# Turning the token rows of the expert pairs on VectorE and through DRAM instead of on TensorE

## The chip, the core and the metric

The kernel runs on one core of a Trainium2 chip. A core has five engines that run side by side, each with an instruction queue of its own that is worked off in order: TensorE (PE, matmuls; PEld is its loading of the stationary operand), VectorE (DVE), ScalarE (ACT), GpSimd (POOL) and SyncE (SP), which here only issues transfers. Transfers (DMAs) are issued from SP, ACT or POOL, are cut into packets, and are carried by 16 DMA engines that all queues share. A queue's next instruction waits until the semaphores it names have come; so a transfer that waits holds up every transfer issued behind it from the same engine.

The metric is the device time of one launch in microseconds (us), as the median of several runs. All numbers are f32.

## The reference

One block of a gated cross-attention network over 32 sequences of 112 rows (3,584 tokens of width 256):

```python
x = x + tanh(g_xattn) * xattn(ctx_1024, layernorm(x))      # 16 heads of 64, keys: 375 context rows and the 112 own ones
x = x + tanh(g_ffn) * moe(layernorm(x))

def moe(x):                                                # D = 256, F = 1024, E = 8 experts
    s = softmax(x @ gate_w); top2, idx = top_k(s, 2); top2 = top2 / sum(top2)
    h = gelu(einsum('td,edf->etf', x, w1) + b1)
    y = einsum('etf,efd->etd', h, w2) + b2
    return sum over the two chosen experts of top2 * y
```

The kernel does not compute all experts for all tokens: it routes each token to its two experts and computes only these.

## The kernel before, in words

**Attention first.** The first 1,440 us or so are the attention of the 32 sequences, with the gate's scores and the routing of the tokens woven in. Every routed row (a token, once per chosen expert, with its weight and its number behind its 256 values: `C` = 260 columns) is scattered to the DRAM table `xg`, which holds one region per expert. During attention, GpSimd also forms sums and differences of the experts' weights and writes them to DRAM (`ws1`, `ws2`; `piece_in`, `piece_sums`, `piece_out`).

**Then the experts.** The rows of the table are worked off in units. `PAIRS` = 21 units are pairs of 128 rows of one expert (`EARLY` = 13 of them can be located before the last tokens are routed, `LATE` = 8 after), and at least `SURE` = 18 more are single blocks of 128 rows. A pair is two Strassen products: `hidden_pair` (seven products of eight 128x128 matmuls: rows times w1) and `second_pair` (seven such products with w2). Both take half matrices and their sums as operands, so a pair needs the weights `w11`, `s23`, `s1`, `12_22`, `s4` for the first layer and `b11`, `b2x`, `t14`, `t32` for the second, 3.5 MB together. Each has one buffer. A transfer into it is issued from SP (`fetch_first`, `fetch_second`) as soon as the products that read the old weights are done, and it is skipped on the chip when the next pair is of the same expert (the condition `cond`).

**The order is written out by hand.** Each engine's instructions stand in the order in which the Python code calls them. In the loop at lines 1852 to 1875, iteration `t` has, in this order: `hidden_pair(t)`; `fetch_first(t + 1)`; the turning of the next pair's rows, `turn_rows(t + 1)`; `rows_sums(t + 1)` (four differences on GpSimd, tile `xt`); a share of the late routing (`pieces_of`, mostly VectorE); `hidden_sums(t)`; `second_pair(t - 1)` and `out_pair(t - 1)`, whose rows are added to the output by GpSimd's indirect DMAs; `fetch_second(t)`; and `rows_ahead(t)`, which fetches the rows `xs` of pair t + 3 from the table, from SP or (later) from ACT.

**What is turned.** `xs` has a row per partition. As an operand of a product, D must lie on the partitions. `turn_rows` (line 1153) makes `xsT` with four TensorE transposes per pair (two halves of D, two blocks; line 1158) into a PSUM bank, and one copy from there to SBUF, by ScalarE in this loop (line 1162). With this layout, partition p of half k holds column k * 128 + p, and the rows of w1 lie in the same way ("(k p)" in the transfers' patterns).

Attention already has another way to turn rows, for its inputs: `turn_inputs` (32x32 blocks turned by VectorE, line 382), `send_inputs` (to the DRAM tile `turned_in`) and `take_inputs` (back, in runs of 32 values, so that the blocks land turned as a whole; line 397).

The functions that the change touches, and what calls them:

Of the kernel before, what the change touches and what calls it, by code (L numbers as in the profile page):

```python
# [23 lines left out]
def kernel(  # L24
# [20 lines left out]
    nc = tc.nc  # L45
# [79 lines left out]
    turned = [dram.tile([QB, QW, QB, 2 * NCK * 2 * QW], F32, name=f"turned_{n}") for n in range(4)]  # L125
    b1d = dram.tile([E, P, NF], F32, name="b1d")
# [74 lines left out]
    if True:  # L201
# [877 lines left out]
        def half_of_w1(e, k, h):  # L1079
            return w1[bass.ds(e, 1), k * P : (k + 1) * P, h * 512 : (h + 1) * 512].rearrange(  # L1080
                "o p f -> p (o f)"
            )

        def rows_of_w1(e, k):
            return w1[bass.ds(e, 1), k * P : (k + 1) * P].rearrange("o p (h f) -> p (o h) f", h=2)

        def columns_of_w1(e, h):
            return w1[bass.ds(e, 1), :, h * 512 : (h + 1) * 512].rearrange(
                "o (k p) f -> p (o k) f", p=P
            )  # L1090
# [54 lines left out]
        def weights_ahead():  # L1145

            pool = ctx.enter_context(tc.tile_pool(name="wexp", bufs=1, side="right"))
            found["w1"] = pool.tile([P, KD, FF], F32, name="w1_0")
            e, _ = expert_of(0)
            fetch_biases(0, e, pool, 1)  # L1150
            nc.sync.dma_start(found["w1"], w1[bass.ds(e, 1)].rearrange("o (k p) f -> p (o k) f", p=P))

        def turn_rows(t, copy=None):
            n = 2 if t < PAIRS else 1
            ps = psum(KD, n, P)
            for k in range(KD):
                for b in range(n):
                    nc.tensor.transpose(ps[:, k, b, :], xs[t][:, b, k * P : (k + 1) * P], ident)
            xsT[t] = found["tiles" if t > 0 else "early"].tile(
                [P, KD, 2, P], F32, tag="xsT", name=f"xsT_{t}"  # L1160
            )
            (copy or nc.vector.tensor_copy)(xsT[t][:, :, :n, :], ps)

# [248 lines left out]
        def piece_in(n):  # L1412
# [4 lines left out]
            if l == 0:  # L1417

                for h in range(2):
                    lo = h * 512 + c * P  # L1420
                    src = w1[e, :, lo : lo + P].rearrange("(k p) f -> p k f", p=P)
# [430 lines left out]
        for t in range(1, PAIRS):  # L1852
            if t > 1:
# [4 lines left out]
                turn_rows(t + 1, nc.scalar.copy)  # L1858
                if t + 1 < PAIRS:
                    rows_sums(t + 1)  # L1860
            pieces_of(shares.pop(0) if shares else 0)
# [7 lines left out]
            if t + AHEAD == EARLY:  # L1869
                do(outgoing)  # L1870
                del outgoing[:]
            rows_ahead(t)
# [69 lines left out]
```

## Time and profile before

| | |
|---|---|
| median of 3 runs | 1870.04 us (1869.91 to 1871.43) |
| the profiled execution | 1871.91 us, its span 1870.2 us |
| PE busy | 1845.6 us, 99% |
| DVE, ACT, POOL busy | 74%, 60%, 52% |
| DMA | 462.51 MB in 389,747 packets, 247 GB/s on average |
| stage of the pairs | from 1452 us (`hidden_pair(1)`) to 1720 us |
| stage of the single blocks | from 1720 us to the end |

The profile divides the span into 40 slices of 46.8 us; the digit of a slice is a busy share in tenths. DMA's share is the time that packets took, summed over the 16 engines and divided by 16 times the width of the slice; packets of one engine can overlap, so it can be above 1. A timeline line names the start, the duration, the engine, the line of the code, the operation, the tiles (written, then read) and their count, and in square brackets the idle time ahead of it and what ended it. Line numbers are those of the kernel before; behind the change they are a little higher. Iteration t of the pairs' loop is told in the text by the start of `hidden_pair(t)`.

### The profile page before, as it was taken

How to read it: one execution, taken by the hardware profiler on the slowest of the kernel's cores; microseconds unless marked ns; L12 is line 12 of the kernel's file. 1: busy time of each engine (PE TensorE's matmuls, PEld its weight loads, DVE VectorE, ACT ScalarE, POOL GpSimd, SP SyncE). 2: the span in 40 equal slices, each digit the busy share in tenths (PEclk: the TensorE clock that was granted, in tenths of full speed). 3: DMA queues.
4: the chain of work that ended last, by engine and by line, in shares of the span. 5: the costliest groups of instructions: out<-in, count | busy, mean ns of one | idle time of the engine just before them, and what ended most of it. 6: DMA issues, size and time to landing. Idle time of an engine off the chain costs nothing. (4 is left out here: it accounts for less than half of the span.)

```text
span 1870.2 us, 37202 instructions
## 1 busy us (share of the span) xinstructions
PE 1845.6 (99%) x12336; PEld 1410.7 (75%) x12336; DVE 1377.5 (74%) x2898; ACT 1131.2 (60%) x2718; POOL 968.0 (52%) x1359
## 2 busy tenths in 40 slices
PE   8999999999999999999999999999999999999998
PEld 4776777676777677766777777767676999999897
DVE  6888887878887878787878787887776477854111
ACT  4776666756776767666767676666756334344333
POOL 6434342525354846484556655662334588877212
PEclk9999999999999999999999999999999999999999
DMA  6577767666878897989898988887547886897872
GB/s 208 204 244 251 247 215 236 228 211 215 261 263 266 285 288 269 289 280 293 280 282 280 284 279 288 266 300 235 217 171 254 265 242 174 263 349 221 247 201 42
DMA packets 389747, 462.51 MB, mean 247 GB/s; under 512 B 142984, under 2 KB 279472, under 8 KB 373168
## 3 DMA queue, kind: packets, MB, share of 16 engines
q1 hardware_dynamic: 359568, 432.19, 69.6%
q0 software_dynamic: 11328, 15.33, 4.3%
q10 hardware_dynamic: 18656, 12.58, 2.5%
q8 instruction: 99, 1.62, 0.3%
q14 instruction: 96, 0.79, 0.1%
HBM read 316.05 MB, written 186.96 MB: 269 GB/s over the span
## 5 line engine op out<-in xcount | busy, mean ns | idle before, releaser
L592 ACT ACTIVATE ex<-bank,nmx 128x512 f32<-128x512 f32 x512 | 344.0, 698 | 85.0 <-DVE nmx L583 85.0
L606 ACT ACTIVATE ex<-ex,rc 128x512 f32<-128x512 f32 x512 | 345.1, 730 | 59.5 <-DVE rc L603 58.8
L583 DVE TENSOR_REDUCE nmx<-bank 128x1 f32<-128x487 f32 x512 | 298.3, 655 | 73.3 <-PE bank L573 72.8
L611 DVE STREAM_TRANSPOSE ex<-ex 128x1024 f32<-128x1024 f32 x256 | 314.4, 1228 | 20.4 <-ACT ex L606 20.0
L524 POOL TENSOR_TENSOR vv<-tmpv,vv 128x512 f32<-128x512 f32 x64 | 81.9, 1280 | 407.2 <-ACT vv L512 396.4
L573 PE MATMUL bank<-kT,qTs 64*128 64x487 f32 x1024 | 234.4, 584 | 1.2 <-ACT outT L652 0.8
L635 PEld LDWEIGHTS bank<-exT,vv 128*64 128x64 f32 (+1 forms) x4096 | 197.5, 136 | 33.2 <-issue 24.8
L652 ACT COPY outT<-bank 128x256 f32<-128x256 f32 (+3 forms) x160 | 40.0, 314 | 296.0 <-PE bank L635 291.5
L635 PE MATMUL bank<-exT,vv 128*64 128x112 f32 (+1 forms) x4096 | 212.0, 260 | 3.0 <-DMA exT<-turned 3.0
L471 PE MATMUL bank<-tT,wkv_s 128*128 128x487 f32 x378 | 186.5, 576 | 0.5 <-ACT ex L592 0.5
L476 PE MATMUL bank<-wkv_s,tT 128*128 128x256 f32 x768 | 186.5, 379 | 0.0
L476 PEld LDWEIGHTS bank<-wkv_s,tT 128*128 128x128 f32 x768 | 145.8, 190 | 44.0 <-issue 22.1
L1452 POOL TENSOR_TENSOR piece<-piece 128x128 f32<-128x128 f32 x256 | 116.8, 456 | 113.9 <-DMA piece<-in_L_ffn_w_dram 102.7
L573 PEld LDWEIGHTS bank<-kT,qTs 64*128 64x128 f32 x1024 | 98.3, 186 | 96.6 <-issue 70.0
L1207 POOL DMA_INDIRECT out_dram<-y,xs x60 | 93.5, 1558 | 146.2 <-DVE y L1234 63.2
L476 PEld LDWEIGHTS bank<-wkv,kvT 128*128 128x128 f32 x512 | 95.8, 190 | 56.5 <-issue 33.5
L476 PE MATMUL bank<-wkv,kvT 128*128 128x256 f32 x512 | 131.8, 380 | 0.8 <-ACT ex L592 0.6
L471 PE MATMUL bank<-kvT,wkv 128*128 128x487 f32 x252 | 130.1, 598 | 0.0
L521 DVE TENSOR_TENSOR vv<-bank,vv 128x512 f32<-128x512 f32 x192 | 123.6, 669 | 7.7 <-POOL vv L524 7.7
L521 DVE TENSOR_TENSOR kT<-bank,kT 128x487 f32<-128x487 f32 x189 | 116.9, 640 | 15.5 <-PE bank L471 12.7
L1262 ACT ACTIVATE h<-h,b 128x256 f32<-128x256 f32 x160 | 66.0, 495 | 91.4 <-DVE h L1275 64.5
L410 PEld LDWEIGHTS bank<-kvT,wq_sb 128*128 128x128 f32 x512 | 96.8, 190 | 28.1 <-issue 17.0
(299 smaller groups left out, 3654.3 us busy)
## 6 DMA issues: line engine op xcount, KB each, us to landing
turned<-ex SPq DMA_DIRECT2D x128, 1024.0 KB
exT<-turned SPq DMA_DIRECT2D x128, 1024.0 KB
w_t<-ws SPq DMA_DIRECT2D x40, 512.0 KB
w<-in_L_ffn_w_dram SPq DMA_DIRECT2D x38, 512.0 KB
w_b2x<-in_L_ffn_w_dram SPq DMA_DIRECT2D x38, 512.0 KB
ws<-piece SPq DMA_DIRECT2D x64, 256.0 KB
turned_in<-inputs SPq DMA_DIRECT2D x28, 512.0 KB
kvT<-turned_in SPq DMA_DIRECT2D x224, 64.0 KB
```

What stands on the lines that cost most here:

```text
L410: nc.tensor.matmul(ps, lhsT=wq_sb[:, k, i * P : (i + 1) * P], rhs=kvT[g][:, k, :, :S], start=(k == 0), stop=(k == KD - 1),)
L471: nc.tensor.matmul(ps, lhsT=w[:, 0, i * P : (i + 1) * P], rhs=x[:, :NK], start=True, stop=True)
L476: nc.tensor.matmul(ps[:, c, :], lhsT=x[:, (2 * h + c) * P : (2 * h + c + 1) * P], rhs=w[:, 1, i * P : (i + 2) * P], start=True, stop=True,)
L521: nc.vector.tensor_tensor(v[o], ps, v[r], ALU.add)
L573: nc.tensor.matmul(ps[:, :NK], lhsT=qT[b // 2, i][r, b % 2].rearrange("p a i -> p (a i)"), rhs=kT[b, i][r, :], start=True, stop=True,)
L583: nc.vector.tensor_reduce(nmx[b, i][:, j : j + 1], pss[b, i][j][:, :NK], AX.X, ALU.max, negate=True)
L592: nc.scalar.activation(exs[n % EXB][:, :, p, :, j, :], ps[j].rearrange("p (c r k) -> p k c r", c=NCK, r=QW), AF.Exp, bias=nmx[b, i][:, j : ...
L606: nc.scalar.mul(t, t, rc[:, j : j + 1])
L611: nc.vector.transpose(t, t)
L635: nc.tensor.matmul(ps[y * DH : (y + 1) * DH, r, x * S : (x + 1) * S].rearrange("p (a i) -> p a i", a=QB), lhsT=vv[j // 2, c // 2][:m, c % ...
L1207: add = nc.gpsimd.indirect_dma_start(out=outf, out_offset=bass.IndirectOffsetOnAxis(ap=xs[t][:, b, D + 1 : D + 2].bitcast(I32), axis=0), i ...
L1452: nc.gpsimd.tensor_tensor(o, l, r, op) for o, l, r, op in ops
```

## The change

For the pairs from t = 3 on, the rows are turned in two steps, two iterations ahead. `turn_ahead(t + 2)` turns the 32x32 blocks of both row blocks with two VectorE instructions into a new tile `ahead` and stores it in one of three new DRAM tiles `rows_in`. `take_ahead(t + 2)`, issued behind `fetch_second(t)`, loads it back into `xsT` with two transfers, one per half k, in runs of 32 values. `turn_rows` stays for pairs 0 to 2 and for the single blocks.

In the new layout, partition p of half k holds column 2p + k of D. The transfers of w1 therefore take its rows two to a partition ("(p k)" instead of "(k p)"), in the pieces for the sums too, and the remaining TensorE transposes read every second column of `xs`.

```diff
+    rows_in = [dram.tile([2, QB, QW, D], F32, name=f"rows_in_{n}") for n in range(3)]
...
         def half_of_w1(e, k, h):
-            return w1[bass.ds(e, 1), k * P : (k + 1) * P, h * 512 : (h + 1) * 512].rearrange(
-                "o p f -> p (o f)"
-            )
+            return w1[bass.ds(e, 1), :, h * 512 : (h + 1) * 512].rearrange(
+                "o (p k) f -> k p (o f)", k=KD
+            )[k]
 
         def rows_of_w1(e, k):
-            return w1[bass.ds(e, 1), k * P : (k + 1) * P].rearrange("o p (h f) -> p (o h) f", h=2)
+            return w1[bass.ds(e, 1)].rearrange("o (p k) (h f) -> k p (o h) f", h=2, k=KD)[k]
 
         def columns_of_w1(e, h):
             return w1[bass.ds(e, 1), :, h * 512 : (h + 1) * 512].rearrange(
-                "o (k p) f -> p (o k) f", p=P
+                "o (p k) f -> p (o k) f", p=P
             )
...
-            nc.sync.dma_start(found["w1"], w1[bass.ds(e, 1)].rearrange("o (k p) f -> p (o k) f", p=P))
+            nc.sync.dma_start(found["w1"], w1[bass.ds(e, 1)].rearrange("o (p k) f -> p (o k) f", p=P))
...
-                    nc.tensor.transpose(ps[:, k, b, :], xs[t][:, b, k * P : (k + 1) * P], ident)
+                    nc.tensor.transpose(ps[:, k, b, :], xs[t][:, b, k:D:KD], ident)
...
+        def turn_ahead(t):
+            n = 2 if t < PAIRS else 1
+            v = found["tiles"].tile([P, 2, D], F32, tag="ahead", name=f"ahead_{t}")
+            for b in range(n):
+                nc.vector.transpose(
+                    v[:, b], xs[t][:, b, :D].rearrange("p (r f k) -> p f k r", k=KD, r=QW)
+                )
+            nc.sync.dma_start(
+                rows_in[t % 3][:n].rearrange("b s j n -> (s j) b n"), v[:, :n]
+            )
+
+        def take_ahead(t):
+            n = 2 if t < PAIRS else 1
+            xsT[t] = found["tiles"].tile([P, KD, 2, P], F32, tag="xsT", name=f"xsT_{t}")
+            src = rows_in[t % 3][:n].rearrange("b s j (f k r) -> k (j f) (b s) r", f=QB, k=KD)
+            for k in range(KD):
+                nc.sync.dma_start(
+                    xsT[t][:, k, :n].rearrange("p b (s r) -> p (b s) r", r=QW), src[k]
+                )
...
-                    src = w1[e, :, lo : lo + P].rearrange("(k p) f -> p k f", p=P)
+                    src = w1[e, :, lo : lo + P].rearrange("(p k) f -> p k f", p=P)
...
                 fetch_first(t + 1)
                 if t + 1 < PAIRS:
                     found["next", t + 2] = expert_of(t + 2)
-                turn_rows(t + 1, nc.scalar.copy)
                 if t + 1 < PAIRS:
                     rows_sums(t + 1)
+                else:
+                    turn_rows(t + 1, nc.scalar.copy)
+            if t + 2 < PAIRS:
+                turn_ahead(t + 2)
             pieces_of(shares.pop(0) if shares else 0)
             hidden_sums(t)
             if t > 1:
                 second_pair(t - 1)
                 out_pair(t - 1)
                 fetch_second(t)
...
+            if t + 2 < PAIRS:
+                take_ahead(t + 2)
             rows_ahead(t)
```

## The prediction

> **What bounds the kernel now.** I read the page's busy shares and slices first, then TensorE's timeline in the stage of the pairs, then the busy time per pair, then the waits.
>
> ```profile
> PE 1845.6 (99%) x12336; PEld 1410.7 (75%) x12336; DVE 1377.5 (74%) x2898; ACT 1131.2 (60%) x2718; POOL 968.0 (52%) x1359
> PE   8999999999999999999999999999999999999998
> DMA  6577767666878897989898988887547886897872
> ```
>
> PE is busy in every slice. The pairs are slices 32 to 37 of 40 (46.8 us each); DMA's digits there are 8, 8, 6, 8, 9, 7, so the shares differ within the stage, and it has to be read period by period.
>
> PE's timeline, one period of the pairs (iterations 6 and 7):
>
> ```profile
> start us, us, engine line op out<-in xcount [idle before <-releaser]
> 1531.10 1.06 PE L1255 MATMUL bank<-xsT,w_s 128*128 128x128 f32 x8
> 1531.99 0.60 PE L1158 MATMUL bank<-ident,xs 128*128 128x128 f32 x4
> 1532.43 1.06 PE L1317 MATMUL bank<-w_b,h 128*128 128x128 f32 x8
> ...
> 1538.68 1.06 PE L1255 MATMUL bank<-xsT,w 128*128 128x128 f32 x8
> ...
> 1544.04 1.06 PE L1255 MATMUL bank<-xsT,w_s 128*128 128x128 f32 x8
> 1544.93 0.60 PE L1158 MATMUL bank<-ident,xs 128*128 128x128 f32 x4
> ```
>
> No line has a wait in brackets, and none has from 1472 to 1730 us: PE goes without a gap. From one group of transposes to the next is 12.94 us, and from their start to the next operation 0.44 us, although they are "busy" for 0.60: the pipeline overlaps, so 0.44 is what they cost PE.
>
> Next the busy time in windows of one period each, which show what else could end the period:
>
> ```profile
> core 0: us, PE busy (x) PEld busy (x) DVE busy (x) ACT busy (x) POOL busy (x), PEclk, DMA share, GB/s
> 1589.00:1602.00 13.00, 13.00 (x118) 12.93 (x117) 11.76 (x27) 4.89 (x13) 11.89 (x13) 1.00 0.71 204
> 1602.00:1614.90 12.90, 12.90 (x118) 12.90 (x117) 11.07 (x27) 6.02 (x16) 10.60 (x12) 1.00 0.83 229
> 1614.90:1627.80 12.90, 12.90 (x118) 12.90 (x117) 10.34 (x26) 5.28 (x15) 9.94 (x11) 1.00 0.89 277
> 1627.80:1640.80 13.00, 13.00 (x119) 13.00 (x118) 7.14 (x15) 4.82 (x13) 9.55 (x10) 1.00 1.09 362
> 1640.80:1653.70 12.90, 12.90 (x118) 12.90 (x117) 7.14 (x15) 4.44 (x12) 9.81 (x10) 1.00 1.05 340
> 1653.70:1666.70 13.00, 13.00 (x119) 13.00 (x118) 7.05 (x15) 6.74 (x18) 10.61 (x12) 1.00 1.08 355
> 1666.70:1679.60 12.90, 12.90 (x118) 12.90 (x117) 7.05 (x15) 5.27 (x15) 9.88 (x11) 1.00 1.07 351
> 1679.60:1692.60 13.00, 13.00 (x119) 13.00 (x119) 7.04 (x15) 5.38 (x15) 10.05 (x11) 1.00 1.07 345
> 1692.60:1705.50 12.90, 12.90 (x118) 12.90 (x117) 7.05 (x15) 5.27 (x15) 9.91 (x11) 1.00 0.89 249
> ```
>
> The columns are PE, PEld, DVE, ACT and POOL busy, the clock, DMA's share and GB/s. The clock is full. The period from 1602 is iteration 12, nearly. From 1628 to 1693 us, five periods (iterations 14 to 18), DMA's share is 1.05 to 1.09 at 340 to 362 GB/s, without a hole: in these the weights of a new expert come for every pair. Before and behind it is 0.71 to 0.89, and down to 0.52 in earlier periods where pairs of the same expert skip their loads. So in these five periods two things are at their limit at once: PE, and the transfers, which keep up by a narrow lead. By the trace's packet records, the 512 packets of 1 KB of `b2x` end 1.4 to 2.7 us before its first product starts there; in iterations 5 and 6 it is 4.0 to 4.2 us.
>
> **The change part by part.**
>
> *PE and ACT, removed.* 18 pairs (t = 3 to 20) lose their transposes: 18 x 0.44 = 7.9 us of PE, all of it on the path as long as PE goes without a gap. 18 copies of 0.56 us leave ACT, 10.1 us, and one PSUM bank per pair; PE waited for neither, so I count nothing. A wait of POOL's for these copies (2.7 us in all) goes too, off the path.
>
> *DVE, added.* 36 block turns of 128x256. The nearest row is L611, 128x1024 in 1,228 ns, a quarter of which is 0.31 us; the new ones read with a stride of 32 bytes, which that row does not, so the bounds are 0.31 and 1.23 us; I take 0.35, as the engine and the operation are the same. That is 0.7 us per pair, behind `hidden_pair`'s last addition. What covers it:
>
> ```profile
> DVE ex L1337 <- PE bank L1317: 28.4, 17, 2.0
> ```
>
> DVE idles 28.4 us over 17 pairs, 1.7 us each, for PE's second group of products (0.58 us at the least, at 1591.6, where routing fills DVE). So 0.7 us hides in all periods but one or two. Behind DVE's row of additions stands a chain: L1343 to POOL's two output DMAs and three sums (L1301), which PE reads 1.3 us after they end in iteration 11 (1601.98 to 1603.32). Without the transposes PE comes 0.44 us earlier. Cost taken: nothing. If a turn takes 1.23 us, 2.5 us per pair stand against some 1.1 us of idle time in a routing period and 0.9 us of POOL's lead: 0.5 us in each of 12 periods, 6 us.
>
> *SP, added.* One store and two loads per pair. The store waits for DVE's turn, and that for `xs[t + 2]`: in iteration 5 its fetch was issued at 1515.5 and its last packet ends near 1520.0, just as DVE comes free at 1520.1, so DVE may wait about a microsecond there, under its idle time. Queued behind the store are `b11` and `b2x`; `b11` is needed a period later, and `b2x` waits for PE until 5 us after the store. The loads wait for the store, issued 6 us before them; queued behind them are the next pair's `w11` to `s4`. Issuing: `kvT<-turned_in`, 512 packets, takes 0.61 us (median), so two of 1,024 packets some 2.4 us, and the store 0.43. `w11` was issued 3.4 us into iteration 5 and is needed 9.5 us after; 2.4 us of delay leave 7. Nothing, where the transfers are not full.
>
> *DMA, added.* Each pair stores 256 KB in 256 packets of 1 KB, and loads them in 2,048 packets of 128 bytes. The nearest row for those is `take_inputs`, in a window of 1 us (1303 to 1304) in which almost nothing else ran:
>
> ```profile
> q1 hardware_dynamic: 1685, 0.21, 135.6%
> ```
>
> 1,685 packets, 0.21 MB: 210 GB/s, against some 350 for the weights. 1.356 x 16 us / 1685 = 12.9 ns of an engine each. At that rate 2,048 take 1.2 us of all engines; bursts of 4,096 took 3.3 us by the packet records, so 1.7; I take 1.6, as bursts are what is added. The store at 350 GB/s takes 0.75 us. So 2.35 us per pair; bounds are 1.5 (both by their bytes) and 3.7 (each small packet at 24 ns, the 99th percentile of those in attention).
>
> VectorE: DVE Perf Modes of the Trainium skill, section "Rules for kernel authors", speaks against this step: it gives a 128x128 transpose to TensorE, and its section on the three transpose paths calls a plain strided DMA 19 times slower than the transposing one (1.31 us for 128x128 bf16), an estimate of 100 us per pair, or over 1 ms in all. The window above shows 1,685 runs of 128 bytes in 1 us, and the burst's 1.7 us gives the sum below; the page's case, a large innermost stride, is not this one, where 32 values are contiguous.
>
> *Where that lands.* Before iteration 13 DMA has room: 0.83 x 12.9 + 2.5 = 13.2 busy us in a period of 12.50, share 1.06. The heavy early one (1485 to 1498, share 0.95) comes to 1.19, is 1.3 us over, and has 4 us of lead. From iteration 13 on, with 1.08 as the ceiling (13.5 busy us in 12.50) and 2.5 busy us added: 1614.9: 11.5 + 2.5, 0.5 over; then 14.2, 13.5, 14.0, 13.8 and 13.9, each + 2.5: 3.2, 2.5, 3.0, 2.8 and 2.9 over. Sum 14.9 busy us, over 1.08 = 13.8 us. Of that, some 1.0 us is taken from the lead; the least lead, 1.4 us, is not all usable, as the landing has still to be told. So PE waits 12.8 us that it did not wait before. In period 1692.6 only the last load is left, and it fits.
>
> *The rest.* The remaining 48 transposes read every second column. LDWEIGHTS of `xs` is 142 ns; bounds are 0 and twice that, 48 x 0.142 = 6.8 us. I take 0, as it lies under the matmuls. w1's rows in another order have packets of the same 2 and 4 KB; the first pair's 4 KB become 8 KB (159 ns against 315), no difference.
>
> *Sum:* -7.9 + 12.8 = +4.9 us on the profiled execution's 1871.9, 1876.8. That execution is 1.9 above the median, so 1875.0 by the runs. By the same working the wait is 7.8 us with 1.5 us added per pair, and 21 with 3.7: a result between 1870 and 1883.
>
> **The rivals.**
>
> *A, above:* 1875, between 1870 and 1883.
>
> *B, the transfers are hidden: faster.* A share of 1.07 is not a measured ceiling: packets overlap, and the small ones reach 1.36. If the engines carry more by overlapping, PE stays without a gap: 1870.0 - 7.9 = 1862. For it: PE never waits, and with only small packets in flight the share is above 1.3. Against it: no hole in 65 us, and a lead of half its size elsewhere. It decides at the ceiling: with 1.14 instead of 1.08 the wait is 7.9 us and equals the gain, and with 16.7 / 12.5 = 1.34 nothing waits.
>
> *C, the early pairs wait too.* The store stands in SP's queue ahead of `b11` and `b2x`, the loads ahead of `w11` to `s4`, and POOL's chain has 1.3 us of lead. Any of these that costs 0.6 us in 18 periods adds 11 us: 1886. For it: SP waits 65.6 us for PE before `fetch_second` and goes straight on, so it has no spare time at that point. Against it: 7 us are left ahead of `w11`.
>
> *D, the strided LDWEIGHTS shows:* up to 6.8 us more, 1882; nothing in the trace speaks for it.
>
> **How the numbers follow.** Chances: A 0.55, B 0.15, C 0.25, D 0.05. 1875 is A's. Within 0.2% (3.7 us, about what a measurement can tell from no change) means 1866.3 to 1873.8. A lies above this in two parts of three (0.37), in it for the rest (0.18); C and D are slower but for 0.03; B is faster but for 0.02. Slower 0.64, same 0.23, faster 0.13. The range 1863 to 1886 leaves out most of B and almost half of C, 0.2 together.
>
> **What the profile after would show.** Periods of 12.50 us up to iteration 12, then 14 to 15.5 us in iterations 13 to 18, PE's waits there being for DMAs of `w_b2x`, `w_t` or `w`, with a share of 1.07 or more. In B, no bracket in PE's timeline and 12.50 throughout. In C, waits before 1600 us. It would be wrong if the loads are quicker in between other transfers than in bursts, or if the turn is slow.

## The result: 1921.2 us, 2.6% slower

The median is 1921.2 us (1915.9 to 1925.2 in 6 runs) against 1871.3 us for the kernel before (1869.9 to 1873.5 in 6 runs on the same chip). The ratio is 1.0259, with a 95% interval of 1.0246 to 1.0271. The prediction was 1875.0 us, within 1863 to 1886: the sign was right, the size was missed by 46 us. The profiled execution took 1920.9 us, with a span of 1919.2 us.

The page of the kernel after, with the busy shares and the slices of PE and DMA (48.0 us each):

```profile
PE 1853.0 (97%) x12264; PEld 1410.4 (73%) x12264; DVE 1384.7 (72%) x2934; ACT 1123.8 (59%) x2700; POOL 967.6 (50%) x1359
PE   8999999999999999999999999999998889779998
DMA  6577767576878897889889898975577887998872
```

PE is no longer busy throughout: its digits fall in slices 31 to 33, 35 and 36, all in the stage of the pairs, and nowhere else. `hidden_pair(1)` starts at 1448.5 us (1452.3 before) and the first single block at 1764.2 (1720.5), so the pairs take 47.5 us longer; from there to PE's end it is 147.3 us (142.2).

PE's timeline, iterations 6 and 7 of the kernel after (in brackets the idle time and what ended it):

```profile
start us, us, engine line op out<-in xcount [idle before <-releaser]
1528.47 1.06 PE L1276 MATMUL bank<-xsT,w 128*128 128x128 f32 x8
1531.62 2.94 PE L1276 MATMUL bank<-xt,w_s 128*128 128x128 f32 x24 [2.10 <-POOL xt L1195]
...
1537.08 1.06 PE L1338 MATMUL bank<-w_b,h 128*128 128x128 f32 x8
...
1544.06 1.13 PE L1276 MATMUL bank<-xsT,w 128*128 128x128 f32 x8 [0.56 <-issue]
```

The transposes are gone, and the products follow each other as before. But one iteration takes 15.6 us where 12.5 were forecast, because PE now stands still: 2.1 us of that for POOL's sums `xt`. POOL came late to these sums. It had sat idle before a scatter of the late routing, until rows `xs` had landed, and the sums stand behind that scatter:

```profile
1529.54 1.01 POOL L822 DMA_INDIRECT xg<-xr,sloti  x1 [6.76 <-DMA xs<-xg]
```

Over the stage, from the second `hidden_pair` to the first single block, PE waits mostly for weights:

```profile
PE bank L1276 <- DMA w_s<-ws: 10.8, 8, 2.1
PE bank L1338 <- DMA w_t<-ws: 8.0, 10, 1.9
PE bank L1276 <- DMA w<-in_L_ffn_w_dram: 4.9, 6, 1.1
PE bank L1276 <- POOL xt L1195: 4.4, 2, 2.3
```

(total us, times, longest). With `w_b2x` (3.4 us) and `w_b` (3.2) the weights' rows come to 30.3 of 38.5 us. The kernel before has no wait of PE's in this stage.

The busy time in windows of one period each, iterations 11 to 16 of the kernel after (columns: PE, PEld, DVE, ACT and POOL busy, the clock, DMA's share and GB/s):

```profile
core 0: us, PE busy (x) PEld busy (x) DVE busy (x) ACT busy (x) POOL busy (x), PEclk, DMA share, GB/s
1602.70:1617.80 15.10, 12.78 (x114) 12.59 (x114) 13.96 (x40) 4.84 (x12) 13.54 (x17) 1.00 0.63 167
1617.80:1631.90 14.10, 12.96 (x115) 12.64 (x113) 10.77 (x28) 5.06 (x12) 11.62 (x12) 1.00 0.92 233
1631.90:1649.30 17.40, 13.76 (x113) 12.89 (x113) 9.57 (x26) 4.95 (x12) 9.73 (x10) 1.00 0.93 268
1649.30:1667.10 17.80, 14.14 (x113) 13.02 (x113) 8.38 (x17) 5.06 (x12) 9.79 (x11) 1.00 1.01 284
1667.10:1685.00 17.90, 14.25 (x114) 13.08 (x114) 8.50 (x17) 5.06 (x12) 9.70 (x11) 1.00 0.98 274
1685.00:1703.70 18.70, 13.69 (x114) 12.81 (x113) 9.31 (x21) 4.95 (x12) 10.60 (x11) 1.00 0.97 289
```

Two things contradict the prediction. The period of iteration 11 is 15.1 us with DMA's share at 0.63: PE waits where transfers have room. And in iterations 13 to 16 the periods are 17.4 to 18.7 us, but DMA's share is 0.93 to 1.01 at 268 to 289 GB/s, where the kernel before held 1.05 to 1.09 at 340 to 362 GB/s. The DMA engines are less full than before, and PE waits all the same. This points to something that is late before it reaches them. The clock is 1.00 in all these windows (0.997 over the whole execution, 0.999 before), so it is not that.

The queue that issues the transfers shows it. SP's timeline in iteration 4 of the kernel before, from `fetch_second` on, and then in iteration 3 of the kernel after (duration is the time that SP needs to issue):

```profile
1500.28 0.47 SPq L1135 DMA_DIRECT2D w_t<-ws  x2
1501.35 0.39 SPq L1053 DMA_DIRECT2D xs<-xg  x1
1502.08 0.34 SPq L1119 DMA_DIRECT2D w<-in_L_ffn_w_dram  x1
1502.76 1.73 SPq L1119 DMA_DIRECT2D w_s<-ws  x2
```

```profile
1485.53 0.37 SPq L1136 DMA_DIRECT2D w_t<-ws  x1
1486.92 1.30 SPq L1181 DMA_DIRECT2D xsT<-rows_in  x2
1488.51 3.84 SPq L1120 DMA_DIRECT2D w<-in_L_ffn_w_dram  x1
1492.69 1.08 SPq L1120 DMA_DIRECT2D w_s<-ws  x2
...
1496.31 0.39 SPq L1172 DMA_DIRECT2D rows_in<-ahead  x1
```

Before, `w11` is issued in 0.34 us. After, the same instruction behind the two loads takes 3.84 us, and everything behind it on SP comes that much later, up to the store, which falls to the end of the iteration.

Where SP waits, over the stage of the pairs (total us, times, longest), before and after:

```profile
engine line waited for: us in total, times, longest us
SPq L1135 <- PE bank L1317: 65.6, 22, 4.9
SPq L1119 <- PE bank L1255: 22.9, 34, 1.8
SPq L1135 <- DMA w<-in_L_ffn_w_dram: 8.2, 10, 1.4
```

```profile
engine line waited for: us in total, times, longest us
SPq L1181 <- DMA rows_in<-ahead: 21.9, 12, 3.4
SPq L1120 <- DMA b<-b1d: 18.8, 6, 6.4
SPq L1120 <- PE bank L1338: 17.2, 12, 4.1
SPq L1136 <- DMA b<-in_L_ffn_b_dram: 8.7, 7, 2.0
```

Before, SP mostly waited for PE to release a weight buffer: it was early. After, it mostly waits for transfers to land. The second row is strange: L1120 is `fetch_first`, and the weights do not depend on `b1d`'s biases, another tile on another engine's queue. The kernel as built explains it (below, in the experiments).

### The profile page after: what moved, and what is told of

Its sections match the earlier page's. It is cut to its first block, busy times and chain, and to the rows that moved or that the text cites. A ratio compares the mean times of both kernels' runs of the same rounds, so it can differ in the third digit from the quotient of the medians.

```text
span 1919.2 us, 37155 instructions
## 1 busy us (share of the span) xinstructions
PE 1853.0 (97%) x12264; PEld 1410.4 (73%) x12264; DVE 1384.7 (72%) x2934; ACT 1123.8 (59%) x2700; POOL 967.6 (50%) x1359
## 5 line engine op out<-in xcount | busy, mean ns | idle before, releaser
L477 PEld LDWEIGHTS bank<-wkv_s,tT 128*128 128x128 f32 x768 | 145.9, 190 | 44.0 <-issue 22.3
L522 DVE TENSOR_TENSOR kT<-bank,kT 128x487 f32<-128x487 f32 x189 | 116.9, 640 | 15.6 <-PE bank L472 13.6
```

Of the source, the lines that this page charges most:

```text
L477: nc.tensor.matmul(ps[:, c, :], lhsT=x[:, (2 * h + c) * P : (2 * h + c + 1) * P], rhs=w[:, 1, i * P : (i + 2) * P], start=True, stop=True,)
L522: nc.vector.tensor_tensor(v[o], ps, v[r], ALU.add)
```

## The experiments

The theories at the start: *engine time* (the packets' time on the DMA engines, the prediction's), *SP's order* (loads wait for the store's landing, ahead of the weights), *many packets* (2,048 of them hold SP at the issue behind), *VectorE* (it waits for `xs` fetched late), *layout*. During the work two more came up: *reader* (POOL and PE wait for a late `xsT`) and *number of transfers*.

All ratios are to the kernel before on the same chip. "us" is the ratio less 1, times 1871.3, so that runs of different chips can be compared.

| run | what it is | median us | ratio, 95% interval | us over before |
|---|---|---|---|---|
| the change | | 1921.2 | 1.0259 (1.0246 to 1.0271) | +48.5 |
| x10_strided | before, strided transposes | 1872.7 | 0.9996 (0.9986 to 1.0007) | -0.7 |
| x1_layout | new layout, PE turns all | 1875.7 | 1.0022 (1.0012 to 1.0032) | +4.1 |
| x2_store | x1 + VectorE's turns and store | 1878.8 | 1.0043 (1.0025 to 1.0062) | +8.0 |
| x14_tinyfree | x1 + 2 tiny free transfers on SP | 1882.3 | 1.0053 (1.0036 to 1.0070) | +9.9 |
| x19_tinyact | x1 + the same 2 on ACT | 1879.5 | 1.0042 (1.0028 to 1.0055) | +7.9 |
| x11_tiny | x2 + 2 tiny loads | 1891.9 | 1.0119 (1.0094 to 1.0145) | +22.3 |
| x12_wideunread | x2 + loads, 256 packets | 1897.4 | 1.0148 (1.0131 to 1.0165) | +27.7 |
| x17_half | x2 + loads, 1,025 packets | 1902.7 | 1.0167 (1.0146 to 1.0187) | +31.2 |
| x18_big | x2 + loads, 512 packets, 512 KB | 1910.1 | 1.0199 (1.0178 to 1.0219) | +37.2 |
| x8_unread | x2 + loads, 2,048 packets | 1919.5 | 1.0248 (1.0231 to 1.0265) | +46.4 |
| x3_wide | the change, 256 packets | 1895.3 | 1.0135 (1.0114 to 1.0156) | +25.3 |
| x4_nowait | the change, no wait for the store | 1919.7 | 1.0255 (1.0237 to 1.0274) | +47.7 |
| x6_xsfirst | the change, rows ahead of loads | 1918.2 | 1.0253 (1.0235 to 1.0270) | +47.3 |
| x5_late | the change, loads behind the weights | 1921.7 | 1.0267 (1.0250 to 1.0284) | +50.0 |
| x9_act | the change, loads on ACT | 1931.0 | 1.0330 (1.0312 to 1.0347) | +61.8 |
| x13_one | the change, one load | 1917.6 | 1.0248 (1.0231 to 1.0265) | +46.4 |
| x16_merge | x13 + s4 and s1 in one transfer | 1912.0 | 1.0213 (1.0193 to 1.0233) | +39.9 |
| x7_early | the change for pairs 3 to 12 only | 1888.8 | 1.0106 (1.0074 to 1.0138) | +19.8 |

### The layout alone

`x1_layout` keeps the new patterns of w1 and the strided transposes, and takes the turning through DRAM out:

```diff
+                turn_rows(t + 1, nc.scalar.copy)
                 if t + 1 < PAIRS:
                     rows_sums(t + 1)
-                else:
-                    turn_rows(t + 1, nc.scalar.copy)
-            if t + 2 < PAIRS:
-                turn_ahead(t + 2)
...
-            if t + 2 < PAIRS:
-                take_ahead(t + 2)
```

> The weights' rows two to a partition and the strided reading of TensorE's transposes alone: all pairs are still turned by TensorE, nothing goes through rows_in. Layout theory (strided loads of weights, strided transposes cost): some of the loss is here, 1875 to 1878 us where each transposed block pays the bound of the prediction, and the singles' 147.3 us stay (142.2 before). All others: as before, 1870 to 1873 us, and the whole 50 us lie in the turning.

`x10_strided` is the kernel before with the transposes' stride alone:

```diff
-                    nc.tensor.transpose(ps[:, k, b, :], xs[t][:, b, k * P : (k + 1) * P], ident)
+                    nc.tensor.transpose(ps[:, k, b, :], xs[t][:, b, k:D:KD], ident)
```

> The kernel before, with its weights' rows as they were, but TensorE's transposes read every second number of the rows (so the products are of wrong features). Strided reading costs: 1873 to 1878 us, as the layout's 1875.7. The rows two to a partition cost (longer packets' time: 94.2 ns against 90.7 for 2 KB in the pairs): 1870 to 1872, no change.

The strided transposes are free (0.9996, and the interval ends at 1.0007). So the 4.1 us (2.2 to 6.0) of `x1_layout` belong to w1's rows two to a partition. That is a small part of the loss, but it was forecast as nothing. The traces do not say how it comes about: in `x1_layout` the single blocks take 147.7 us against 142.2 before (144.2 in `x10_strided`), with more waits for weights, but the packets of 2 KB take 99.8 ns there, 98.6 in `x10_strided` and 96.6 before, which settles nothing. This stays open.

### The parts of the turning, added one by one

In this series TensorE goes on turning all pairs and computes with that, so nothing waits for the new path. What is lost is lost by the load that the path puts on the engines and queues. `x2_store` adds VectorE's turns and the store to `x1_layout`:

```diff
+            if t + 2 < PAIRS:
+                turn_ahead(t + 2)
```

> The new layout, all pairs turned by TensorE, and beside that VectorE's two turns (0.61 us each in the profile after) and the store to rows_in; the two loads are left out (nobody reads rows_in). Engine time: 0.75 us of packets a pair in the six full iterations, under 5 us more than the layout alone, 1871 to 1876. SP's order and many packets: next to nothing, since what blocks SP are the loads, 1871 to 1876 too. VectorE theory (its turns wait for rows fetched two iterations ahead and hold up its other work): a good part of the loss is here, 1885 to 1905.

`x8_unread` adds the loads too, at their place, into a tile that nobody reads:

```diff
-            xsT[t] = found["tiles"].tile([P, KD, 2, P], F32, tag="xsT", name=f"xsT_{t}")
+            v = found["tiles"].tile([P, KD, 2, P], F32, tag="ahead", name=f"taken_{t}")
...
-                    xsT[t][:, k, :n].rearrange("p b (s r) -> p (b s) r", r=QW), src[k]
+                    v[:, k, :n].rearrange("p b (s r) -> p (b s) r", r=QW), src[k]
```

> The new layout, TensorE turns all pairs and its xsT is what is computed with; VectorE's turns, the store and the two loads of 1,024 packets each stand where they stand in after, but the loads go into a tile that nobody reads. Queue theory (what the loads do to SP and to the transfers behind them): the loss stays, and with the 7.9 us of TensorE's turns on top, 1915 to 1930 us. Reader theory (the sums of POOL and so TensorE wait for xsT that lands late; 38.5 us of POOL waits in after): the loss goes, 1879 to 1890.

The store and VectorE cost 3.9 us together, with intervals that overlap. The loads cost 38.4 us more, although nobody reads them: the reader theory falls as the main cause. (The tile that nobody reads takes one of the two buffers of `ahead`. In none of the runs of this series does VectorE wait for the store or for these loads in its rows of waits.) This run also shows where the 7.9 us of PE went: PE does the transposes here and not in the change, and the times are 1919.5 and 1921.2 us. PE does not set the period any more, so what it saves is lost in its waits.

What of a load costs? `x11_tiny` leaves two transfers of one packet at that place, `x12_wideunread` carries all bytes in 256 packets of 1 KB, `x17_half` half of the small packets, `x18_big` twice the bytes in 512 packets of 1 KB:

```diff
-            src = rows_in[t % 3][:n].rearrange("b s j (f k r) -> k (j f) (b s) r", f=QB, k=KD)
+            src = rows_in[t % 3].rearrange("b s j n -> b (s j) n")
             for k in range(KD):
-                nc.sync.dma_start(
-                    v[:, k, :n].rearrange("p b (s r) -> p (b s) r", r=QW), src[k]
-                )
+                nc.sync.dma_start(v[:1, k].rearrange("p b r -> p (b r)"), src[k, :1])   # x11_tiny
+                nc.sync.dma_start(v[:, k].rearrange("p b r -> p (b r)"), src[k])        # x12_wideunread
```

```diff
+            nc.sync.dma_start(v[:, 0, :n].rearrange("p b (s r) -> p (b s) r", r=QW), src[0])   # x17_half
+            nc.sync.dma_start(v[:1, 1, 0], rows_in[t % 3][0, 0, :1, :P])
...
+            src = rows_in[t % 3].rearrange("b s j n -> (s j) b n")                             # x18_big
+            w = found["tiles"].tile([P, KD, 2, P], F32, tag="more", name=f"more_{t}", bufs=1)
+            for v in (v, w):
+                nc.sync.dma_start(v.rearrange("p k b r -> p k (b r)"), src)
```

> As the kernel with unread loads (TensorE turns all, VectorE turns and stores too; 1919.5 us), but each of the two loads takes one packet of 1 KB, and the rest of the pair's rows is not loaded: number, place and wait of the transfers stay, their bytes and packets go. Number of transfers (two more instructions on SP a pair, the wait for the store, and transfers that wait for an earlier one's turn to end): most of the 41 us stays, 1900 to 1920. Bytes or packets: 1878 to 1884, as with the store alone (1878.8).

> As the kernel with unread loads (1919.5 us), but the same 256 KB go in 256 packets of 1 KB and not in 2,048 of 128 B. Number of packets: 1879 to 1887. Bytes: 0.8 us of engine time a pair, so about half of the 41 us stays, 1895 to 1905. Number of transfers: 1915 to 1920.

> As the kernel with unread loads, but the first load alone is whole (1,024 packets of 128 B, 0.84 us of engine time); the second takes one packet. The wide unread loads (256 packets, 0.8 us of engine time) took 1897.4 us, the full ones (2,048 packets, 1.7 us) 1919.5, the tiny ones 1891.9. DMA engines' time: as the wide ones, 1895 to 1899. Number of packets (SP held behind them): midway or more between the tiny and the full ones, 1904 to 1910. A ring that takes the first thousand at once and holds SP only beyond: 1892 to 1897 and no issue of SP over 1 us.

> As the kernel with unread loads, but each of the two loads takes the whole 256 KB of the pair in 256 packets of 1 KB (50 ns each): 512 packets and 1.6 us of engine time a pair, against 2,048 packets and 1.7 us in the kernel with unread loads (1.0248 times before) and 256 packets and 0.8 us in the wide one (1.0148). Engine time: as with the many packets, 1.022 to 1.026 times before. Number of packets: near the wide one, 1.013 to 1.018.

No single theory survives, and each has a part. Two transfers of one packet cost 14.3 us over the store alone, which lies between the two expectations. The bytes of the rows, in few packets, add 5.4 us, with intervals that overlap. From there to 2,048 packets it is 18.7 us, and `x18_big` splits that in two: the engines' time of the many packets, with twice the bytes in a quarter of their number, costs 9.5 us (its interval meets neither that of the wide loads nor that of the many packets), and the number itself the other 9.2 us. As the bytes double in `x18_big`, the 9.5 us do not tell engine time from bytes. `x17_half` fits neither number it was to tell apart: +31.2, and its interval overlaps that of the wide loads. By itself it was inconclusive, but it speaks against its third theory, that the first thousand packets hold nothing: 9 of SP's issues take over 1 us there.

The part that is due to the number of packets can be read on SP. After the same two loads, `w11` in `x8_unread` (2,048 packets) and in `x18_big` (512 packets, as much engine time):

```profile
1486.08 1.26 SPq L1181 DMA_DIRECT2D taken<-rows_in  x2
1487.63 4.29 SPq L1120 DMA_DIRECT2D w<-in_L_ffn_w_dram  x1
```

```profile
1488.75 0.40 SPq L1182 DMA_DIRECT2D taken<-rows_in  x1
1489.19 0.49 SPq L1182 DMA_DIRECT2D more<-rows_in  x1
1489.97 0.36 SPq L1120 DMA_DIRECT2D w<-in_L_ffn_w_dram  x1
```

It is 4.29 us against 0.36. The Trainium skill, page "Perfetto Trace Analysis", section "DMA Instruction — HWDGE (DVE, Sync)", says that the time shown of such an instruction ends only after all its descriptors have been generated, and that a descriptor buffer can fill up meanwhile. An instruction that is slow because of those ahead of it would fit that, but no run here shows the buffer or its size.

### Two tiny transfers

Why would two packets of 1 KB cost 14 us? `x14_tinyfree` issues them at the same place without a store, from an input, so that no data makes them wait; `x19_tinyact` issues the same two from ACT (there `nc.scalar`):

```diff
+        def tiny(t):
+            v = found["tiles"].tile([P, KD, 2, P], F32, tag="ahead", name=f"tiny_{t}")
+            for k in range(KD):
+                nc.sync.dma_start(v[:1, k].rearrange("p b r -> p (b r)"), w1[0, k : k + 1, : 2 * P])
...
+            if t + 2 < PAIRS:
+                tiny(t + 2)
```

> The new layout, all pairs turned by TensorE, no turn of VectorE, no store; at the place of the two loads SP issues two transfers of one packet of 1 KB each from an input (nothing to wait for, nobody reads them). Number of transfers (each transfer of SP or ACT first waits until the eighth before it has landed, and two more a pair bring that nearer): most of the 13 us shows here, 1884 to 1890 us against 1875.7. Wait for the store: nothing, 1875 to 1878.

> As the kernel with two free tiny transfers a pair (1.0053 times before; the layout alone 1.0022), but ACT issues them and not SP. The ring that SP and ACT share: as from SP, 1.004 to 1.007. SP's own time (its issues and what stands behind them): as the layout alone, 1.001 to 1.003.

From SP they cost 5.8 us over the layout, 40% of the 14.3 us that they cost behind a store; what the store adds to their price, no run splits. From ACT it is 3.8, which is just within what the shared ring was expected to give, but the interval reaches into the other expectation. The traces say more than the times. In `x14_tinyfree` PE waits for weights (four rows, 4.1 us in all; 0.4 us in `x1_layout`). In `x19_tinyact` it waits for no transfer, but for ACT, whose copies stand behind the tiny transfers (`xsT` 1.6 us, `h` 0.6 us), and ACT idles 6.5 us until tiny ones have landed. So the two runs cost about the same by different ways, and what holds the tiny transfers on both engines can be seen in the kernel as built. SP's transfers of one iteration of `x14_tinyfree`, in order, with the semaphores that each waits for (an instruction's number, its line, what it moves):

```
1119 L1136 DMACopy w_t<-ws 128x2x512 [waits DMAHW5]
1120 L1188 DMACopy tiny<-in_L_ffn_w_dram 1x256 [waits DMAHW6]
1121 L1188 DMACopy tiny<-in_L_ffn_w_dram 1x256 [waits DMAHW7]
1124 L1054 DMACopy xs<-xg 128x2x260 [waits DMASW4,DMASW1,DMASW5,DMASW0,DMAHW1,DVE,Activation]
1126 L1120 DMACopy w<-in_L_ffn_w_dram 128x512 [waits DMAHW2,PE]
1128 L1120 DMACopy w_s<-ws 128x2x512 [waits DMAHW3,PE]
```

The tiny transfers depend on nothing, and still wait. The semaphores DMAHW0 to 7 are given to the transfers of SP and ACT in turn, and each transfer waits until the one eight before it has landed. So at most eight of SP's and ACT's are under way, and two more per pair bring every wait nearer. Rows of such waits move to the top of SP's waits, first in `x14_tinyfree`, then in `x11_tiny`:

```profile
SPq L1120 <- DMA w_t<-ws: 22.2, 13, 3.3
SPq L1136 <- PE bank L1343: 19.9, 13, 4.6
SPq L1136 <- DMA b<-b1d: 19.6, 7, 5.8
```

```profile
SPq L1120 <- DMA b<-b1d: 33.9, 10, 6.7
SPq L1120 <- DMA w_t<-ws: 28.7, 15, 4.4
SPq L1136 <- DMA b<-in_L_ffn_b_dram: 14.1, 6, 4.4
```

`fetch_first` does not depend on `w_t` or `b1d`; it waits for their turn of a semaphore. No run changes the number of these semaphores by itself. Summed over SP's rows of waits in the stage of the pairs (from the second `hidden_pair` to the first single block), and over its issues (the columns do not fill the stage: register loads, and waits of other kinds, are not in them):

| | stage, us | SP waits for PE | SP waits for landings | SP issues, us | issues over 1 us |
|---|---|---|---|---|---|
| before | 248.1 | 88.7 | 31.7 | 50.4 | 2 |
| x1_layout | 250.0 | 76.1 | 51.6 | 51.8 | 2 |
| x2_store | 251.7 | 33.8 | 79.8 | 58.9 | 2 |
| x14_tinyfree | 256.1 | 30.2 | 88.3 | 60.8 | 1 |
| x19_tinyact | 254.1 | 68.1 | 56.6 | 50.5 | 1 |
| x11_tiny | 267.1 | 16.2 | 101.2 | 70.3 | 4 |
| x12_wideunread | 270.2 | 12.4 | 107.2 | 74.0 | 2 |
| x17_half | 274.0 | 14.6 | 94.3 | 85.8 | 9 |
| x18_big | 287.1 | 11.8 | 105.4 | 76.0 | 1 |
| x8_unread | 292.8 | 20.4 | 63.6 | 126.8 | 22 |
| the change | 295.4 | 26.2 | 73.6 | 132.5 | 23 |

Read from top to bottom this is the loss. SP's wait for PE was its reserve, 88.7 us in 19 iterations or 4.7 us in each: while SP waits for PE, its transfers go out the moment a buffer comes free. From the kernel before to `x12_wideunread`, SP waits about as long in all (113.6 to 127.7 us, for PE and landings together). But waits for PE have become waits for landings, and these end after the buffer has come free. The first additions on SP eat two thirds of the reserve and cost little (`x2_store`, `x14_tinyfree`). With the reserve gone, the stage gets longer: first through waits for landings (`x11_tiny`, `x12_wideunread`, and `x18_big` with fuller engines), then also through issues that are held (`x17_half`, `x8_unread`, the change). This reading is argued from the sums. `x19_tinyact` does not fit it: there the reserve stays at 68.1 us and ACT is what is held.

Where in time the loss lies is told by the starts of `hidden_pair`. Of the 19.0 us by which the stage of `x11_tiny` is longer than before, 14.3 lie in iterations 13 to 18, the ones that the prediction took as full. What the many packets add (`x8_unread` over `x12_wideunread`, 22.6 us) lies to more than half, 12.7 us, in iterations 2 to 12.

### Taking single causes out of the change

```diff
-            src = rows_in[t % 3][:n].rearrange("b s j (f k r) -> k (j f) (b s) r", f=QB, k=KD)
+            src = rows_in[t % 3].rearrange("b s j n -> b (s j) n")                          # x3_wide
...
-                rows_in[t % 3][:n].rearrange("b s j n -> (s j) b n"), v[:, :n]
+                rows_in[t % 2 + 1 if t > 3 else 0][:n].rearrange("b s j n -> (s j) b n"), v[:, :n]   # x4_nowait
-            src = rows_in[t % 3][:n].rearrange(
+            src = rows_in[0][:n].rearrange(
...
+            rows_ahead(t)                                                                   # x6_xsfirst
             if t + 2 < PAIRS:
                 take_ahead(t + 2)
-            rows_ahead(t)
...
                 fetch_first(t + 1)                                                          # x5_late
+                if 2 < t + 1 < PAIRS:
+                    take_ahead(t + 1)
...
-            if t + 2 < PAIRS:
-                take_ahead(t + 2)
```

> As after, but the two loads take the same 256 KB in 256 packets of 1 KB (50 ns each in the trace after, 0.8 us on 16 engines) and not in 2,048 of 128 B (13.2 ns, 1.7 us); the numbers land in the wrong places, so the products of pairs 3 to 19 are of wrong rows. Wait and place in the queue stay. Many packets (they hold the issue of the next transfer on SP for 3 to 4 us): most of the loss goes, 1870 to 1885. Engine time: 0.9 us a pair less, 18 x 0.9 = 16 us at the most, 1905 or more. SP's order (wait for the store's landing): little changes, 1905 to 1918.

> As after, but all loads read the first of the three DRAM tiles, which is stored once (pair 3), and the stores of later pairs go to the other two: the same bytes and packets at the same place, with no store to wait for; pairs 4 to 19 are computed from the rows of pair 3. SP's order by way of the wait (21.9 us of SP waits at the loads): most of that comes back, 1895 to 1902. Many packets, engine time: the wait turns into the same wait behind the packets, 1912 to 1921.

> As after, but the transfer of the rows of pair t + 3 is issued ahead of the two loads and not behind them. VectorE theory (waits of up to 9.1 us for these rows, 17.5 us in all, and POOL's 12.5 us for them): most of that comes back, 1895 to 1905 us. Queue theory: only the iterations in which SP fetches rows change, under 6 us, 1915 to 1922.

> As after, but the two loads of pair t + 1 are issued one iteration later, behind the five weight transfers of fetch_first(t + 1) and no longer ahead of them; the rows' transfer of SP thus stands ahead of the loads too. Queue theory: the weights are early again and the waits for w_s, w_t and xs go; what is left is the engine time in the full iterations and xsT that lands some 3 us before its sums, 1875 to 1895 us. Reader theory: the loads are later than before, so the sums of POOL are later and it gets slower than after, 1925 to 1950. Engine time alone: 1915 to 1925, no change.

Wide loads bring 23 us back, as in the series above (the change +48.5, `x3_wide` +25.3; unread +46.4 and +27.7). Nothing is gained by leaving out the wait for the store (`x4_nowait`), nothing by fetching the rows first (`x6_xsfirst`): 21.9 us of SP's waits and 17.5 us of VectorE's, both large rows, were consequences. `x5_late` puts the weights ahead of the loads and is not faster either; only the theory of engine time alone had expected that. There the weights are on time (PE waits 0.3 us for them, 30.3 in the change) and the loads are late:

```profile
POOL xt L1195 <- DMA xsT<-rows_in: 76.8, 30, 7.5
```

The change has 38.5 us, 17 times, in this row. In these two orders the queue needs the same time, and the order only chooses who waits.

```diff
-                nc.sync.dma_start(                                       # x9_act
+                nc.scalar.dma_start(
                     xsT[t][:, k, :n].rearrange("p b (s r) -> p (b s) r", r=QW), src[k]
...
-            for k in range(KD):                                          # x13_one, x16_merge
-                nc.sync.dma_start(
-                    xsT[t][:, k, :n].rearrange("p b (s r) -> p (b s) r", r=QW), src[k]
-                )
+            nc.sync.dma_start(
+                xsT[t][:, :, :n].rearrange("p k b (s r) -> p k (b s) r", r=QW), src
+            )
...
-                s1_, s4_ = (                                             # x16_merge
-                    (n, ws1[bass.ds(e, 1), place].rearrange("o p f -> p (o f)"))
-                    for n, place in (("s1", 3), ("s4", 2))
-                )
+                s41 = "s41", ws1[bass.ds(e, 1), 2:4].rearrange("o s p f -> p (o s) f")
```

> As after, but the two loads are issued by ACT, in ACT's own queue, at the same place in the program. If what costs is that SP itself is held behind the loads: SP's weights are early again, and what is lost is ACT's own time (its wait for the store, 3 to 4 us, ahead of its next Gelus, of which 8 us a pair were idle), 1875 to 1900 us. If what costs is shared by the queues (the DMA engines' order, or whatever makes the packets): 1910 to 1930.

> As after, but the two loads of 1,024 packets each are one transfer of 2,048 packets: same bytes, same packets, same numbers, one instruction less on SP. Number of packets: no change, 1915 to 1923 us. Number of transfers: a third of the added ones goes, 1900 to 1912.

> As the change with one load in place of two (1917.6 us), and the transfers of s4 and s1 are one of 512 KB too: 12 transfers of SP and ACT a pair in place of 13 (after 14, before 11), same bytes and packets. Number of transfers: some 4 to 6 us less, 1910 to 1914. Other causes: s4's buffer comes free later than s1's, so the merged one is issued later: 1917 to 1925.

On ACT the loads are worse than either expectation. SP's issues fall back to 59.3 us in the stage, only 2 take over 1 us, as before, and it waits instead for the landing of transfers of ACT that its weights do not depend on, while ACT's Gelus stand behind the loads:

```profile
SPq L1120 <- DMA xsT<-rows_in: 74.9, 23, 9.7
```

```profile
ACT h L1286 <- DMA xsT<-rows_in: 57.1, 6, 13.6
```

The Trainium skill, page "DMA: Bandwidth & Descriptors", section "Issuing engines are not separate DMA queues", says that spreading transfers over engines saves only the issuing time, as the same 16 DMA engines carry them. Here SP's issuing time was saved (59.3 us against 132.5), and the kernel became slower.

One load in place of two is 2.1 us better by the ratios, within the intervals. One transfer less again, by merging `s4` and `s1`, is 6.5 us better than that and 8.6 us better than the change (there the intervals do not meet), although `s1` then waits for the buffer of `s4`. That is what the number of transfers predicts, from the other side. The merged transfer also changes the order, `12_22` now going ahead of `s1`, and no run separates the two. (The counts in the expectation leave out the transfer of the rows; their differences are right.)

`x7_early` turns only pairs 3 to 12 in the new way, and leaves pairs 13 to 20 to TensorE:

```diff
+        TURNED = 12
...
+                if t + 1 > TURNED:
+                    turn_rows(t + 1, nc.scalar.copy)
                 if t + 1 < PAIRS:
                     rows_sums(t + 1)
-                else:
-                    turn_rows(t + 1, nc.scalar.copy)
-            if t + 2 < PAIRS:
+            if t + 2 < TURNED + 1:
                 turn_ahead(t + 2)
...
-            if t + 2 < PAIRS:
+            if t + 2 < TURNED + 1:
                 take_ahead(t + 2)
```

> Pairs 3 to 12 are turned as in after and pairs 13 to 19 by TensorE; new layout. The prediction (only iterations 13 to 18, with full transfers, lose; earlier ones gain 0.44 us each): 1871 to 1873 us, the layout's 1876 less 10 x 0.44 = 4.4. Queue theory (every iteration with loads loses): about the 20 us that the periods up to iteration 12 lost in after, 1892 to 1900.

The ten early pairs cost 19.8 - 4.1 (the layout) = 15.7 us, 1.6 us each, where the prediction had a gain. The other eight cost 48.5 - 19.8 = 28.7 us, 3.6 each. No variant comes below the kernel before.

## Why the prediction was wrong

*What failed:* the step on SP, "2.4 us of delay leave 7. Nothing, where the transfers are not full". The 7 us were the distance from the issue of one transfer to its need. The queue's own reserve was less, the 88.7 us that SP spends waiting for PE in 19 iterations, and it had to pay for three added transfers and for what each of them does to the turn of eight: `x2_store` and `x14_tinyfree` show two thirds of it gone by one store or two tiny transfers, and all additions of `x8_unread` together make the stage 44.7 us longer before anything reads their result. The prediction even quotes the larger of the two rows (65.6 us), as a sign that SP has "no spare time at that point". It was the spare time.

*The issue of the loads.* Forecast as 2.4 us per pair, from a row with 512 packets. The two loads themselves take 1.0 to 1.5 us in ten iterations (2.2 to 3.9 in the other eight), and the transfer behind them 2.8 to 4.8 in twelve: SP's issues grow by (132.5 - 50.4) / 18 = 4.6 us per pair. The 0.61 us that was scaled is the median of a row whose longest issue is 4.47 us (shortest, median, longest, in ns):

```profile
L397 SPq DMA_DIRECT2D kvT<-turned_in x224: 337/614/4470, 130.9 to 1305.2; - x112
1286.03 7.69 SPq L397 DMA_DIRECT2D kvT<-turned_in  x8
1299.56 6.11 SPq L397 DMA_DIRECT2D kvT<-turned_in  x8
```

Eight of them, 4,096 packets, held SP for 7.69 and 6.11 us. By these lines 2,048 packets cost 3.1 to 3.8 us and not 2.4: the holding could be read in the kernel before.

*Where the waits come* was right in part. The change loses 26.1 us in iterations 13 to 18, where the prediction had a wait of 12.8 us, and PE's waits are for the weights that it named, and for `w_s`. But it loses 18.3 us in iterations 2 to 12 too, where the prediction had only a gain.

*DMA's price* was right and not the point. The packet records of the 18 pairs show 1.65 to 1.78 us of all engines for the 2,048 small packets (forecast 1.6), and in a window of 1 us (1607 to 1608) that holds nothing but them:

```profile
q1 hardware_dynamic: 1280, 0.16, 102.0%
```

That is 1.02 x 16 us / 1,280 = 12.8 ns a packet, as in attention (12.9). The runs show that engine time (or bytes) counts, 9.5 us in `x18_big` for 0.8 us per pair, but not only where the engines are full: of the 16.9 us between the stages of `x12_wideunread` and `x18_big`, 9.2 lie in iterations 2 to 12. The ceiling of 1.08 from which the 12.8 us were worked out was not reached: 0.93 to 1.01.

*PE's gain of 7.9 us* is as said where PE does not wait: from `hidden_pair(10)` at 1590.22 to the next at 1602.73 it is 12.51 us. But other iterations are longer, and so nothing of it is left in the sum (`x8_unread` against the change).

*VectorE's turns* take longer than taken, and lie within the bounds:

```profile
L1169 DVE STREAM_TRANSPOSE ahead<-xs x36: 595/614/648, 1470.1 to 1729.0; 128x256 f32<-128x256 f32 x36
DVE ex L1358 <- PE bank L1338: 25.0, 13, 3.6
```

The idle time that was to cover them (second row, as far as 1720 us) is still there, and turns and store together cost 3.9 us in `x2_store`. The step's zero was at most some us off.

*The rest.* Strided LDWEIGHTS: nothing, as forecast (`x10_strided`); rival D falls. w1's rows, "no difference": 4.1 us. The rule of the Trainium skill that gives a 128x128 transpose to TensorE (VectorE: DVE Perf Modes, "Rules for kernel authors") agrees with the result, as the change is slower, though the cost lies in the queue and not in the turn. The 100 us per pair that were estimated from the same page's factor of 19 are not seen; it is 2.9.

*The rivals.* C ("the early pairs wait too") named the place, SP's queue, and was given a quarter of the chance; its price of 0.6 us per period was free of any row. Measured against a kernel with the layout and without the 7.9 us of PE, it is (48.5 - 4.1 + 7.9) / 18 = 2.9 us per pair. A's mechanism, full engines in six iterations, is not what the windows show. The range's upper end was C at 0.6 us, so it could not hold the result. The profile after shows what was named for C: waits before 1600 us.

## What to carry to other kernels

Before adding transfers to a queue, add up how long that queue waits for buffers to come free: this is its reserve per iteration, and here it, not the distance of one transfer to its need, paid for further transfers. Take the price of an issue from the time of a whole burst and not from the median of a row. Count transfers as well as bytes, and look in the built kernel at which semaphores they take in turn, for a transfer can wait for another that it has nothing to do with. A load cut into thousands of small packets was paid twice here, in the DMA engines' time and by the next transfer of its queue, whose issue is held; and a large row of waits may be only a consequence, as the wait for the store and the one for the rows were here.

## What was not expected of the hardware

- Behind 2,048 packets of 128 bytes the next transfer's issue took 3.84 and 4.29 us in the lines above; behind 512 packets of 1 KB, with as much engine time, 0.36 us. One load of 2,048 packets holds SP as two of 1,024 do (16 issues over 1 us with a sum of 65.5 us in `x13_one`, 23 with 65.4 us in the change).
- VectorE's turn of 128x256 with a stride in its reading takes 0.61 us, twice the quarter (0.31) of a contiguous 128x1024 one; no run splits that into the stride and a fixed cost per instruction.
- w1's rows two to a partition cost 0.22% in packets of the same sizes, and no trace here says where.
